# Running sums by way of device memory, and other orders for weights, fetches and norms in a two-layer kernel

## Chip, cores and metric

The kernel runs on one core of a Trainium2 chip. The metric is the device time of one execution in microseconds (us), taken as the median of the runs. The profile comes from one further execution of the same program.

## What is computed

Two layers work on x, 2 sequences of 512 tokens with 256 channels, all in float32. In each, x becomes x + s(norm(x)) * silu(f(norm(x))).

- Layer 0, s: a selective state-space scan. A root-mean-square norm and a projection give a gate (512 channels), the scan's input (512), a step width for each of 4 heads, and B and C (128 states). The input passes a causal convolution of width 4. Then, with running sums of the logarithmic decays, `L = exp(cum_i - cum_j)` for i >= j, `y = (L * (C B^T)) (dt x) + exp(cum) C state`, plus `D x`, times silu(gate), and an output projection.
- Layer 0, f: a mixture of 8 experts of which each token takes 2: `silu(x W1) * (x W2)`, then `W3`, weighted by the router's softmax.
- Layer 1, s: causal attention with 32 query heads, 8 key and value heads of 64 channels, and rotary positions.
- Layer 1, f: `sign(norm * gamma + beta)` times the signs of centred weights, plus a bias, times alpha.

## The kernel before

Tokens lie in 8 tiles of 128, 4 to a sequence (`b` is the sequence, `i0` the tile in it, `t` both). The program is one long order written out by hand (`manual_schedule`): each helper adds its instructions to the queues of the engines at the place where it is called, and each engine takes its own in that order. SyncE (SP) issues nearly all plain transfers and GpSimd (POOL) the indirect ones, each in order, so an issue that waits holds up those behind it.

*Layer 0.* After norms, routing and the first features (to about 40 us) the order mixes the experts with the scan. An expert ("unit") takes 256 token slots. Its rows are gathered from `rows` (`expert_slots`, L563), transposed (`expert_turned`, L594), multiplied by both up-projections in three calls of `expert_hidden` (L612) and projected by `expert_end` (L637), whose rows GpSimd scatters to the table `chosen` (L575). `weights_of(e)` asks for the up-projections `w` (two buffers, L358 and L359), `last_weights_of(e)` for `wp` (one buffer, L365). Before, `last_weights_of(e)` and `weights_of(e + 1)` are called behind `expert_end(e - 1)`. Tokens beyond the 256 of a unit go into an overflow block (`rests(0)`, the steps `next(few)`): its weights come as "pieces" by indirect gathers on GpSimd (L563), four to a piece, and are used in L707 and L739.

The scan goes by tile: `spread`, `decays`, `weighed`, `within`, `out_of`. `running_sums` makes the sums `cum` with one matmul of `la` (tokens by heads) by a triangle of ones (L444). `decays` needs the sums of a tile along the free axis, the same on all partitions. Before, `spread` multiplies the triangle by `la` on VectorE (L458, 128x512, two buffers `rl`), and a matmul by a matrix of ones adds the rows into PSUM:

```python
cps = bank_b()
cumb = heads(cps)
PE.matmul(cps, lhsT=ones, rhs=parts[t].rearrange("p h n -> p (h n)"), start=True, stop=True)
```

ScalarE (L471) and VectorE (L478, L481) read that. `spread` is called one to two tiles ahead of its `decays`.

*The turn* (about 224 to 254 us) leads from layer 0 to attention. `gates(1, ...)` (L258, L264) and a product (L1322) finish the scan's output of sequence 1 in `held`; `projected_out` multiplies it (L553), `scanned` adds it (L559). `fetched(b)` asks for the two expert rows of each token (`xn` L1090, `y1` L1091, four transfers of 256 KB on SyncE), `activated` adds them on GpSimd (L1098) and takes the silu on ScalarE (L1099). `residual` makes x and its moments on VectorE (L1104, L1105, L216), `begun1` takes square roots on ScalarE (L197, L198), `normed1_out` the norm on VectorE (L225), `features1` transposes it (L233) and copies it on ScalarE (L1124) to `x1T`. `weights_of_signs` transposes the signs (L1140) and copies them (L1141). `key` and `query` (L1169, rotation on VectorE) and `value` (L1186, copy L1188) follow. Attention's eight PSUM banks take the place of the ones used so far, and so its first scores (L1237) wait until those are free.

*Attention*, from about 254 us, goes head pair by head pair and is not edited.

Of the kernel before, what the change touches and what calls it, by code (L numbers as in the profile page):

```python
# [8 lines left out]
F32 = mybir.dt.float32  # L9
# [14 lines left out]

RESTS = 2 * (B * T - OWN) // REST
BLK = 2 * E + RESTS // RPB
MANY = 3
PIECE = 512
PIECES = 9
# [23 lines left out]
def fused_kernel(  # L53
# [35 lines left out]
    def bank_b():  # L89
        return psum.tile([P, 512], F32, tag="B", name="bank_b")  # L90
# [88 lines left out]
           allow_small_or_imprecise_dtypes=True)  # L179
    rows = dram.tile([B * T, C], F32, tag="rows", name="rows")  # L180
    chosen = dram.tile([2 * B * T, C], F32, tag="chosen", name="chosen")

    first = const.tile([P, NT, E], F32, tag="first", name="first")
    for e in range(E):
# [77 lines left out]
    def gates(b, which=range(NH)):  # L262
        for h in which:
            S.activation(gT[b][:, h, :], features(b, h * P, bank_a()), AF.Silu)  # L264
# [73 lines left out]
    def wide(name, t):  # L338
        return mw.tile([P, NH, P], F32, tag=name, name=f"{name}{t}")
# [16 lines left out]
    def weights_of(e):  # L356
        w = ep.tile([P, WID1], F32, tag="w", name=f"w{e}")
        nc.sync.dma_start(w[:, : 4 * PIECE].rearrange("p (n c) -> p n c", n=4), by_expert[e, :, :4])  # L358
        nc.sync.dma_start(w[:, 4 * PIECE :].rearrange("p (n c) -> p n c", n=2),  # L359
                          by_expert[e, :, 4:6, :384])  # L360
        weights[e] = [w]
# [79 lines left out]
    def running_sums():  # L441

        ps = bank_b()
        PE.matmul(ps[:, : NT * NH], lhsT=upper, rhs=la.rearrange("p t h -> p (t h)"),  # L444
                  start=True, stop=True)
        V.tensor_copy(cum.rearrange("p t h -> p (t h)"), ps[:, : NT * NH])

    def heads(ap):
        return ap.rearrange("p (h n) -> p h n", h=NH)
# [4 lines left out]
    def spread(b, i0):  # L454

        t = b * TPB + i0
        rl = wide("rl", t)
        V.tensor_tensor(rl, upper.unsqueeze(1).to_broadcast([P, NH, P]),  # L458
                        la[:, t, :].unsqueeze(2).to_broadcast([P, NH, P]), ALU.mult)
        parts[t] = rl  # L460

    def decays(b, i0):

        t = b * TPB + i0
        ti = slice(i0 * P, (i0 + 1) * P)

        cps = bank_b()
        cumb = heads(cps)
        PE.matmul(cps, lhsT=ones, rhs=parts[t].rearrange("p h n -> p (h n)"), start=True, stop=True)
        ec = wide("ec", t)  # L470
        S.activation(ec, cumb, AF.Exp)  # L471

        xps = bank_b()
        for h in range(NH):
            PE.transpose(xps[:, h * P : (h + 1) * P], ssmT[b][:, h, ti], ident)
        L = wide("L", t)
        for h in range(NH):
            V.scalar_tensor_tensor(L[:, h, :], cumb[:, h, :], cum[:, t, h : h + 1], negm,  # L478
                                   ALU.subtract, ALU.add)
        dte = mw.tile([P, NH], F32, tag="dte", name=f"dte{t}")  # L480
        V.tensor_tensor(dte, cumb[:, :, P - 1], cum[:, t, :], ALU.subtract)  # L481
        S.activation(L, L, AF.Exp)
        S.activation(dte, dte, AF.Exp)
        xdt = wide("xdt", t)
        V.tensor_tensor(xdt, heads(xps), dt3[:, t, :].unsqueeze(2).to_broadcast([P, NH, P]),
                        ALU.mult)
        parts[t] = ec, L, xdt, dte

    def weighed(b, i0):
        t = b * TPB + i0  # L490
        tk = slice(t * P, (t + 1) * P)
        ec, L, xdt, dte = parts[t]

        cb = bank_b()
        PE.matmul(cb[:, :P], lhsT=BT[:, tk], rhs=CT[:, tk], start=True, stop=True)
        V.tensor_tensor(L, cb[:, :P].unsqueeze(1).to_broadcast([P, NH, P]), L, ALU.mult)
        cs = xe = None
        if i0 < TPB - 1:
            xe = wide("xe", t)
            V.tensor_tensor(xe, xdt, dte.unsqueeze(2).to_broadcast([P, NH, P]), ALU.mult)  # L500
        if i0 > 0:
            cs = wide("cs", t)
            V.tensor_tensor(cs, CT[:, tk].unsqueeze(1).to_broadcast([P, NH, P]), ec, ALU.mult)
        parts[t] = (ec, L, xdt, cs, xe)
# [136 lines left out]
    def within(b, i0):  # L641
        outputs(b, i0)
        passed(b, i0)
        if b == 0:
            gated(b, i0)

    def out_of(b, i0):
        projected_out(b, i0)
        scanned(b, i0)
# [3 lines left out]
    def expert_slots(e):  # L653
        xgs[e] = gathered(e)

    def expert_turned(e):
        xgTs[e] = turned(e, xgs.pop(e))

    def expert_hidden(e, *groups):
        hidden(hids.setdefault(e, []), weights[e][0], xgTs[e], groups, e)  # L660

    def expert_end(e):
        project(e, weights[e], hids.pop(e))
# [95 lines left out]
    with tc.manual_schedule():  # L759
# [163 lines left out]
        convolved(0, 0)  # L923
        gates(0, (1,))
        running_sums()
        gates(0, (2,))
        expert_turned(0)
        expert_slots(1)
        spread(0, 0)
        gates(0, (3,))  # L930

        count = rt("count", [1], mybir.dt.int32)
# [21 lines left out]
        next(few)  # L954
        expert_hidden(1, 0)
        decays(0, 0)
        spread(0, 1)
        expert_end(0)
        last_weights_of(1)
        weights_of(2)  # L960
        weighed(0, 0)
        decays(0, 1)
        expert_hidden(1, 2)
        expert_turned(2)
        expert_slots(3)
        weighed(0, 1)
        within(0, 0)
        spread(0, 2)
        expert_hidden(1, 4)
        expert_hidden(2, 0)  # L970
        within(0, 1)
        decays(0, 2)
        expert_end(1)
        last_weights_of(2)
        weights_of(3)
        out_of(0, 0)
        weighed(0, 2)
        spread(0, 3)
        expert_hidden(2, 2)
        expert_turned(3)  # L980
        expert_slots(4)
        within(0, 2)
        expert_hidden(2, 4)
        decays(0, 3)
        out_of(0, 1)
        expert_hidden(3, 0)
        weighed(0, 3)
        expert_end(2)
        last_weights_of(3)
        weights_of(4)  # L990
        out_of(0, 2)
        conv_in(1, 0)
        within(0, 3)
# [12 lines left out]
        conv_in(1, 3)  # L1006
        convolved(1, 2)
        w_k, cs_t, w_f = early_weights()
        expert_end(3)
        last_weights_of(4)  # L1010
        weights_of(5)
        convolved(1, 3)
        spread(1, 0)
        expert_hidden(4, 2)
        decays(1, 0)
        expert_turned(5)
        expert_slots(6)
        expert_hidden(4, 4)
        next(few)
        weighed(1, 0)  # L1020
        spread(1, 1)
        expert_hidden(5, 0)
        within(1, 0)
        expert_end(4)
        last_weights_of(5)
        weights_of(6)
        next(few)
        decays(1, 1)
        expert_hidden(5, 2)
        weighed(1, 1)  # L1030
        expert_turned(6)
        expert_slots(7)
        expert_hidden(5, 4)
        within(1, 1)
        spread(1, 2)
        expert_hidden(6, 0)
        next(few)
        decays(1, 2)
        expert_end(5)
        last_weights_of(6)  # L1040
        weights_of(7)
        next(few)
        weighed(1, 2)
        expert_hidden(6, 2)
        next(few)
        expert_turned(7)
        spread(1, 3)
        expert_hidden(6, 4)
        next(few)
        within(1, 2)  # L1050
# [31 lines left out]
    w_q = aw.tile([P, KC, PAIRS * P], F32, tag="w_q", name="w_q", bufs=1)  # L1082
    x1 = x_sb

    def fetched(b):

        y1 = aw.tile([P, TPB, C], F32, tag=f"pr{b}", name=f"y1_{b}")
        by_tile = chosen.rearrange("(s p) c -> p s c", p=P)
        for t in range(b * TPB, (b + 1) * TPB, 2):
            nc.sync.dma_start(xn[:, t : t + 2, :], by_tile[:, t : t + 2, :])  # L1090
            nc.sync.dma_start(y1[:, t % TPB : t % TPB + 2, :], by_tile[:, NT + t : NT + t + 2, :])  # L1091
        return y1

    def activated(b, y1):
# [26 lines left out]
        normed(xn, x1, range(b * TPB, (b + 1) * TPB), mvs[b], made["roots", b][:, TPB:])  # L1121

    def features1(b):
        to_features(xn, b, lambda k, ps: S.copy(x1T[:, k, batch(b)], ps))  # L1124


    def signs_of_weights():
# [185 lines left out]

    tc.no_sync_barrier()
    with tc.manual_schedule():
        y1s = [fetched(0)]
        query_weights(0)
        signs_of_weights()
        within(1, 3)
        for h in range(NH):  # L1320
            gates(1, (h,))
            V.tensor_tensor(held[0][:, h, :], held[0][:, h, :], gT[1][:, h, :], ALU.mult)  # L1322
        w_v = mem.tile([P, KC, KV * HD], F32, tag="hT1", name="w_v")
        nc.sync.dma_start(w_v, wv.rearrange("(k p) n -> p k n", p=P))
        late_weights.append(w_v)
        query_weights(1)

        activated(0, y1s[0])
        for i0 in range(TPB):
            projected_out(1, i0)  # L1330
        made["wsT"] = weights_of_signs()
        mvs = [moments_of(0, "ln1")]
        for t in range(TPB):
            residual(t, mvs[0])
        begun1(0)
        normed1_out(0)
        for i0 in range(TPB):
            scanned(1, i0)
        y1s.append(fetched(1))
        features1(0)  # L1340
        activated(1, y1s[1])
        key(0, 0)
        nextq = query(0, 0)
        for i in range(2):
            value(0, i)
        mvs.append(moments_of(1, "ln1"))
# [220 lines left out]
```

## Time and profile before

| | |
|---|---|
| runs | 627.05, 627.86, 630.6 us; median 627.86 |
| profiled execution | 626.98 us, span 625.2 us |
| granted TensorE clock, mean | 0.997 |
| transfers | 45.74 MB; 73 GB/s over the span |
| ones-matmuls of the sums (L469) | 16 records (8 matmuls of two passes), 56.3 to 209.6 us |
| products for them on VectorE (L458) | 8, median 0.684 us |
| `w` transfers (1024 + 384 KB) | 8.9 to 11.8 us from issue to landing |
| `wp` transfers (768 KB) | 4.3 us from issue to landing |

The span runs from the first to the last instruction. PE is TensorE's matmuls and PEld its weight loads, DVE is VectorE, ACT ScalarE, POOL GpSimd; a float32 matmul appears as two records, one for each pass. "A <- B" behind an idle time names what ended it. "issue" is time in which the engine waited for nothing that the profile shows. The granted clock is TensorE's share of its full speed.

### The profile page before, as it was taken

The page shows a single profiled execution, that of the slowest core. Times are in us where ns is not written, and L with a number is a line of the kernel's source. Part 1 is how long each engine was busy: PE and PEld are TensorE (multiplying, and loading weights), DVE is VectorE, ACT ScalarE, POOL GpSimd, SP SyncE. Part 2 cuts the span into 40 slices and gives each one's busy share as a digit, 9 for nine tenths or more (in the row PEclk, how much of TensorE's full clock was granted, in tenths as well). Part 3 has the DMA queues.
Part 4 walks back from the last instruction along what each step waited for, and adds up shares of the span by engine and source line. Part 5 has one row for each costly group of instructions (what it writes and reads, how often), then busy time and mean ns, then how long its engine had stood idle before and what let it go on. Part 6 is the DMA issues. An engine that isn't in the chain of part 4 may idle for free.

```text
span 625.2 us, 11011 instructions
## 1 busy us (share of the span) xinstructions
PE 602.9 (96%) x3847; PEld 410.0 (66%) x3847; DVE 422.7 (68%) x1347; ACT 356.3 (57%) x921; POOL 278.7 (45%) x312
## 2 busy tenths in 40 slices
PE   7999999999998997999899999999999999999997
PEld 5568788777766864465455565666866656666676
DVE  6778654465435336899996889986159888888411
ACT  6443333243331434779888677886048999999610
POOL 3022411354663121575736537474025776666700
PEclk9999999999999998999999999999999999999999
DMA  7710641675856144000000000400000000000000
GB/s 240 266 35 24 230 150 38 221 228 196 282 165 227 72 159 160 2 1 2 1 2 2 0 2 1 135 2 1 18 17 2 2 2 1 3 2 1 2 11 23
DMA packets 24987, 45.74 MB, mean 73 GB/s; under 512 B 2621, under 2 KB 12607, under 8 KB 24928
## 3 DMA queue, kind: packets, MB, share of 16 engines
q1 hardware_dynamic: 19840, 30.71, 14.2%
q0 software_dynamic: 4512, 13.77, 7.2%
q8 instruction: 31, 0.51, 0.3%
q10 hardware_dynamic: 576, 0.52, 0.2%
q14 instruction: 28, 0.23, 0.1%
HBM read 40.80 MB, written 4.33 MB: 72 GB/s over the span
## 4 chain that ended last, share of the span: by engine, by line
PE 48%; DVE 13%; ACT 4%; issue 1%; POOL 1%; DVEq 0%; POOLq 0%; ACTq 0%
PE bank L1296 9%; PE bank L1288 8%; PE bank L1169 7%; PE bank L1276 7%; PE bank L1237 7%; DVE pr L1250 5%; PE bank_a L637 2%; ACT pr L1256 2%; PE bank L1186 1%; POOL pr L1264 1%; PE bank_a L258 1%; DVE sw_q L1159 1%; PE bank_a L612 1%; PE bank_b L553 1%; PE bank L1148 1%
## 5 line engine op out<-in xcount | busy, mean ns | idle before, releaser
L1264 POOL TENSOR_SCALAR pr<-pr,den 128x128 f32<-128x128 f32 (+2 forms) x192 | 193.7, 1024 | 145.1 <-DVE den L1432 145.1
L1256 ACT ACTIVATE pr<-pr,nmax 128x128 f32<-128x128 f32 (+3 forms) x256 | 142.3, 562 | 44.7 <-DVE nmax L1250 43.3
L1250 DVE CUSTOM_DVE_ANT_0 pr<-bank,cmask 128x128 f32<-128x128 f32 (+3 forms) x256 | 109.8, 484 | 11.0 <-PE bank L1237 7.3
L1277 ACT COPY pt<-bank 128x384 f32<-128x384 f32 (+1 forms) x192 | 82.3, 525 | 12.6 <-PE bank L1276 12.6
L1276 PEld LDWEIGHTS bank<-ident,pr 128*128 128x128 f32 x640 | 71.6, 141 | 20.4 <-issue 12.2
L612 PE MATMUL bank_a<-xgT,w 128*128 128x256 f32 x352 | 79.7, 379 | 0.9 <-DMA w<-in_moe 0.9
L1276 PE MATMUL bank<-ident,pr 128*128 128x128 f32 x640 | 75.6, 273 | 2.8 <-DVE oT L1416 2.3
L1288 PE MATMUL bank<-pt,v 128*64 128x384 f32 (+3 forms) x512 | 77.0, 439 | 1.4 <-ACT pt L1277 1.4
L612 PEld LDWEIGHTS bank_a<-xgT,w 128*128 128x128 f32 x352 | 65.5, 190 | 10.4 <-DVE yg L542 1.2
L1237 PE MATMUL bank<-kT,q 64*64 64x128 f32 (+7 forms) x1024 | 69.9, 410 | 0.7 <-ACT v L1188 0.7
L1288 PEld LDWEIGHTS bank<-pt,v 128*64 128x64 f32 x512 | 35.6, 136 | 46.1 <-issue 22.1
L1169 PE MATMUL bank<-x1T,w_q 128*128 128x512 f32 x124 | 61.5, 618 | 0.0
L1296 PE MATMUL bank<-w_o,oT 128*128 128x256 f32 x256 | 56.1, 380 | 0.6 <-DVE oT L1413 0.6
L1296 PEld LDWEIGHTS bank<-w_o,oT 128*128 128x128 f32 x256 | 48.3, 190 | 7.7 <-DVE oT L1413 0.8
L1256 ACT ACTIVATION_READ_ACCUMULATOR pr<-pr,nmax 128x1 f32 x256 | 50.3, 197 | 0.0
L1237 PEld LDWEIGHTS bank<-kT,q 64*64 64x64 f32 x1024 | 38.0, 133 | 14.3 <-issue 5.1
L563 POOL DMA_INDIRECT piece<-in_moe,wrow x36 | 37.4, 1040 | 22.2 <-issue 9.4
L1169 PEld LDWEIGHTS bank<-x1T,w_q 128*128 128x128 f32 x124 | 21.0, 189 | 37.0 <-issue 27.0
L575 POOL DMA_INDIRECT chosen<-o,dest x16 | 16.4, 1024 | 64.7 <-ACT o L574 34.8
L637 PE MATMUL bank_a<-wp,hid 128*128 128x256 f32 x192 | 43.1, 380 | 0.3 <-PEq L1065 0.3
L563 POOL DMA_INDIRECT xg<-rows,tok x16 | 16.7, 1046 | 54.0 <-DVE res L917 29.2
L637 PEld LDWEIGHTS bank_a<-wp,hid 128*128 128x128 f32 x192 | 35.9, 190 | 6.1 <-issue 1.6
(282 smaller groups left out, 794.6 us busy)
## 6 DMA issues: line engine op xcount, KB each, us to landing
w<-in_moe SPq DMA_DIRECT2D x8, 1024.0 KB, 11.8
wp<-in_moe SPq DMA_DIRECT2D x8, 768.0 KB, 4.3
w<-in_moe SPq DMA_DIRECT2D x8, 384.0 KB, 8.9
w_q<-in_wq SPq DMA_DIRECT2D x2, 1024.0 KB
w_o<-in_wo SPq DMA_DIRECT2D x2, 1024.0 KB
rows<-xn SPq DMA_DIRECT2D x4, 256.0 KB, 3.1
xn<-chosen SPq DMA_DIRECT2D x4, 256.0 KB, 2.8
y<-chosen SPq DMA_DIRECT2D x4, 256.0 KB, 3.0
```

The source lines that it names most:

```text
L563: G.indirect_dma_start(out=buf, out_offset=None, in_=src[:, :], in_offset=bass.IndirectOffsetOnAxis(ap=at, axis=0), bounds_check=src.shape ...
L612: PE.matmul(ps[:, i * OWN : (i + 1) * OWN], lhsT=w[:, a : a + P], rhs=xgT[:, k * OWN : (k + 1) * OWN], start=(k == 0), stop=(k == KC - 1))
L637: PE.matmul(ps[:, :C], lhsT=hid[j // 2][:, a : a + P], rhs=wp[:, j * C : (j + 1) * C], start=(j == 0), stop=(j == 5))
L1169: PE.matmul(ps, lhsT=w[:, k, n * P : (n + 1) * P], rhs=x1T[:, k, batch(b)], start=(k == 0), stop=(k == KC - 1))
L1237: PE.matmul(pss[hh][to, a : a + full], lhsT=q[half, n * HD : (n + 1) * HD], rhs=kT[b][half, m, :full], start=True, stop=True)
L1250: V.tensor_tensor_reduce(w["pr"][hh][:, span(i)], w["ps"][i][hh], cmask[:, i & 1, T - (i + 1) * P :], -1.0, 3.0e38, ALU.add, ALU.min, w["n ...
L1256: S.activation(x, x, AF.Exp, scale=-1.0, bias=w["nmax"][hh][:, i : i + 1], accum_out=sum_of(w, i, hh))
L1264: eng.tensor_scalar(x, x, sum_of(w, i, hh), None, ALU.mult)
L1276: PE.transpose(ps[:, col : col + P], pr[hh][:, at : at + P], ident)
L1277: S.copy(pts[hh][:, bank_at[n] : bank_at[n] + widths[n]], ps[:, : widths[n]])
L1288: PE.matmul(pv[hh * HD : (hh + 1) * HD, j * P :], lhsT=v_sb[b][:, j, g * HD : (g + 1) * HD], rhs=pts[hh][:, at : at + w], start=(j == 0), ...
L1296: PE.matmul(ps[:, :C], lhsT=oTs[b][:, c, i * P : (i + 1) * P], rhs=made["w_o"][c // 8][:, c % 8, :], start=(c == 0), stop=(c == PAIRS - 1))
```

## The change

1. The sums of a tile no longer come from VectorE and TensorE. `running_sums` makes them a second time with tile and head on the partitions (32x128) and writes them to a table `cum_rows` in device memory; `spread` reads one row of 512 numbers to all 128 partitions by a transfer on SyncE. `spread` is called two tiles ahead, right behind the `decays` that frees its buffer.
2. `weights_of(e)` is called ahead of `expert_end(e - 2)` instead of behind it and behind `last_weights_of(e - 1)`; `expert_hidden(1, 4)` moves ahead of `weighed(0, 1)` and `within(0, 0)`.
3. In the turn, `fetched(0)` is called behind the first gate, with `y1` on ScalarE's queue; `weights_of_signs` is called ahead of the silus and of `projected_out`; two matmuls of constants, whose result nobody reads, stand behind `projected_out`; `features1(0)` goes ahead of `scanned` and `fetched(1)`, and its second copy to VectorE.

```diff
+KEEP = 2
...
+    cum_rows = dram.tile([NT * NH, P], F32, tag="cum_rows", name="cum_rows")
...
+        PE.matmul(ps[: NT * NH, P : 2 * P], lhsT=la.rearrange("p t h -> p (t h)"), rhs=upper,
+                  start=True, stop=True)
+        by_row = lent("yg", "by_row", P)[: NT * NH]
+        V.tensor_copy(by_row, ps[: NT * NH, P : 2 * P])
+        nc.sync.dma_start(cum_rows[:, :], by_row)
         V.tensor_copy(cum.rearrange("p t h -> p (t h)"), ps[:, : NT * NH])
...
     def spread(b, i0):
         t = b * TPB + i0
-        rl = wide("rl", t)
-        V.tensor_tensor(rl, upper.unsqueeze(1).to_broadcast([P, NH, P]),
-                        la[:, t, :].unsqueeze(2).to_broadcast([P, NH, P]), ALU.mult)
-        parts[t] = rl
+        cumb = wide("rl", t)
+        nc.sync.dma_start(cumb.rearrange("p h n -> p (h n)"),
+                          cum_rows[t * NH : (t + 1) * NH, :].rearrange("a n -> (a n)")
+                          .partition_broadcast(P))
+        parts[t] = cumb
...
     def decays(b, i0):
-        cps = bank_b()
-        cumb = heads(cps)
-        PE.matmul(cps, lhsT=ones, rhs=parts[t].rearrange("p h n -> p (h n)"), start=True, stop=True)
+        cumb = parts[t]
...
         running_sums()
+        spread(0, 0)
+        spread(0, 1)
         gates(0, (2,))
         expert_turned(0)
         expert_slots(1)
-        spread(0, 0)
...
         decays(0, 0)
-        spread(0, 1)
+        spread(0, 2)
+        weights_of(2)
         expert_end(0)
         last_weights_of(1)
-        weights_of(2)
         weighed(0, 0)
         decays(0, 1)
+        spread(0, 3)
         expert_hidden(1, 2)
         expert_turned(2)
         expert_slots(3)
+        expert_hidden(1, 4)
         weighed(0, 1)
         within(0, 0)
-        spread(0, 2)
-        expert_hidden(1, 4)
         expert_hidden(2, 0)
         within(0, 1)
         decays(0, 2)
+        spread(1, 0)
+        weights_of(3)
         expert_end(1)
         last_weights_of(2)
-        weights_of(3)
...
         w_k, cs_t, w_f = early_weights()
+        weights_of(5)
         expert_end(3)
         last_weights_of(4)
-        weights_of(5)
         convolved(1, 3)
-        spread(1, 0)
         expert_hidden(4, 2)
         decays(1, 0)
+        spread(1, 2)
...
-    def fetched(b):
+    def fetched(b, second=nc.sync):
...
             nc.sync.dma_start(xn[:, t : t + 2, :], by_tile[:, t : t + 2, :])
-            nc.sync.dma_start(y1[:, t % TPB : t % TPB + 2, :], by_tile[:, NT + t : NT + t + 2, :])
+            second.dma_start(y1[:, t % TPB : t % TPB + 2, :], by_tile[:, NT + t : NT + t + 2, :])
...
     def features1(b):
-        to_features(xn, b, lambda k, ps: S.copy(x1T[:, k, batch(b)], ps))
+        to_features(xn, b, lambda k, ps: (S.copy, V.tensor_copy)[k if b == 0 else 0](
+            x1T[:, k, batch(b)], ps))
...
     with tc.manual_schedule():
-        y1s = [fetched(0)]
-        query_weights(0)
         signs_of_weights()
         within(1, 3)
         for h in range(NH):
             gates(1, (h,))
+            if h == 0:
+                y1s = [fetched(0, nc.scalar)]
+                query_weights(0)
             V.tensor_tensor(held[0][:, h, :], held[0][:, h, :], gT[1][:, h, :], ALU.mult)
...
         query_weights(1)
+        made["wsT"] = weights_of_signs()
         activated(0, y1s[0])
         for i0 in range(TPB):
             projected_out(1, i0)
-        made["wsT"] = weights_of_signs()
+        ps = bank_a()
+        for _ in range(KEEP):
+            PE.matmul(ps, lhsT=ident, rhs=cmask[:, 0, :], start=True, stop=True)
         mvs = [moments_of(0, "ln1")]
         for t in range(TPB):
             residual(t, mvs[0])
         begun1(0)
         normed1_out(0)
+        features1(0)
         for i0 in range(TPB):
             scanned(1, i0)
         y1s.append(fetched(1))
-        features1(0)
         activated(1, y1s[1])
         key(0, 0)
```

The calls of `spread`, `weights_of`, `expert_end` and `last_weights_of` for the other tiles and units move in the same way.

## The prediction

> **What bounds the kernel.** I read the page's busy table, then TensorE's waits up to the start of attention, then the chain of work that ended last, then the timeline of the turn between the layers.
>
> ```profile
> PE 602.9 (96%) x3847; PEld 410.0 (66%) x3847; DVE 422.7 (68%) x1347; ACT 356.3 (57%) x921; POOL 278.7 (45%) x312
> ```
>
> TensorE is the bound, but an average hides where. Its waits between 20 and 254 us (total, times, longest):
>
> ```profile
> PE bank_a L233 <- issue: 4.1, 1, 4.1
> PE bank_b L739 <- DMA piece<-in_moe,wrow: 1.3, 2, 0.7
> PE bank_a L612 <- DMA w<-in_moe: 0.9, 1, 0.9
> PE bank L1237 <- ACT v L1188: 0.7, 1, 0.7
> ...
> PE bank_b L469 <- DVE rl L458: 0.4, 1, 0.4
> ```
>
> Before the turn (to 238 us) the listed idle time is about 4 us in 218: there, a matmul removed is time saved. In the turn TensorE stands for 4.1 us and waits on chains of other engines. The end of the turn in the chain (start, length, what):
>
> ```profile
> 238.79 0.58 ACT rw L1141
> 239.38 0.01 issue
> 239.38 1.28 ACT L197
> ...
> 242.75 1.98 PE bank_a L233 x8
> 244.73 5.00 PE bank_b L1169 x8
> 249.73 3.45 PE bank_b L1186 x8
> 253.18 0.02 issue
> 253.20 0.59 ACT v L1188
> ```
>
> Four passes should take 1.73 us (a later row of the same line has 1.91), yet the eight at 244.73 took 5.00: the windows (PE, PEld, DVE, ACT, POOL, granted clock, DMA share, GB/s) show why.
>
> ```profile
> 238.00:243.00 5.00, 0.94 (x7) 0.52 (x5) 3.51 (x16) 2.35 (x4) 0.00 (x0) 1.00 0.03 10
> 244.00:247.25 3.25, 3.25 (x8) 1.50 (x6) 0.94 (x3) 1.34 (x3) 0.00 (x0) 0.50 0.50 162
> ```
>
> After the idle stretch the clock is 0.50 from 244.0 to about 247.4.
>
> **Part 1: the sums.** Eight ones-matmuls (L469) go; the chain prices one:
>
> ```profile
> 209.35 0.86 PE bank_b L469 x2
> ```
>
> 8 x 0.86 = **-6.88 us**, all before the turn. The wait in front of one of them (0.42) goes too: **-0.42**. Eight VectorE products (L458, 0.684 us each) go from an engine that is off the path there: nothing. Added in `running_sums`: one matmul of two 128-column passes, 0.22 us by the spacing of the like pairs of L495: **+0.22**. Its 32x128 copy (the 128x32 copy beside it took 0.183) and the 16 KB write are hidden: the write can go at about 40 us, the first broadcast is wanted by `decays(0,0)` at 58, and SyncE issues nothing else between 19 and 62.
>
> The eight broadcasts of 256 KB are in no row of before. Nearest rows: `rows<-xn`, 256 KB, 3.1 us to landing; at the far end the 128 KB scatter at 186.15 that held its successor 7.6 us. I take 3, since shape and size are those of the first. Each is asked for two tiles ahead (`spread(0,2)` after `decays(0,0)`, 61.2, used near 80), so its latency is covered. Each waits on SyncE's queue for the decays that frees its buffer, with the next unit's weights queued behind: that is its real price, counted next. Reading the sums from SBUF instead of PSUM I price at nothing (ScalarE 0.597 from PSUM in L471, 0.630 from SBUF in L482: 8 x 0.03 on an engine with slack).
>
> **Part 2: unit weights sooner.** Before, `w` of unit e went behind `wp` of e-1, which waits for `expert_end`:
>
> ```profile
> 62.94 0.37 SPq L365 DMA_DIRECT2D wp<-in_moe  x1
> 63.42 0.42 SPq L358 DMA_DIRECT2D w<-in_moe  x1
> ```
>
> It was needed at 72.89 and came 0.86 late, 10.3 us after issue. Now it goes behind `spread(0,2)`, at about 61.7; TensorE needs it at 72.89 - 2 x 0.86 = 71.2. 61.7 + 10.3 = 72.0, less what `wp` no longer takes ahead of it. I take **-0.6** (bounds 0 and -0.86). Units 3, 4, 6 and 7 are asked 2.5 to 17 us sooner by the same reading, so they have cover; unit 5 (1.4 MB) stands behind the 0.75 MB that `early_weights` asks for at 132, and is needed at 146.9: 14 us for what the windows there move in 9.
>
> The last pieces of the overflow block waited 0.60 and 0.74 us. GpSimd shows why:
>
> ```profile
> 186.15 1.02 POOL L575 DMA_INDIRECT chosen<-o,dest  x1 [0.30 <-issue]
> 193.76 1.00 POOL L575 DMA_INDIRECT chosen<-o,dest  x1 [6.59 <-issue]
> 195.07 1.04 POOL L563 DMA_INDIRECT piece<-in_moe,wrow  x1 [0.30 <-issue]
> ```
>
> The second scatter waits while the DMA engines are full (share 1.02 from 188 to 192, the weights of unit 7, asked at 184.8), and the last gathers stand behind it. Those weights now move about 17 us earlier: **-1.0** (bounds 0 and -1.34). Against it: gathers of pieces 4 and 5 are eight issues 1.3 us apart from 160.2, and end just in time at 174.7; TensorE now comes 0.86 sooner: **+0.5** (bounds 0 and 0.9). `expert_hidden(1,4)` ahead of `weighed(0,1)` costs nothing: what slides back 2.8 us is first used at 86.4 (L553).
>
> Sum before the turn: -6.88 - 0.42 + 0.22 - 0.6 - 1.0 + 0.5 = **-8.2**.
>
> **Part 3: the turn**, on before's clock.
> - `y` on ScalarE's queue, behind the first gate (ends 226.46). Before, SyncE issued `xn` at 226.17 and `y` only at 227.20; now about 226.95. The two issues (0.4 each) delay the second gate by under 0.3, which the third absorbs. GpSimd's first add (231.82) comes up to 0.5 sooner.
> - The sign transposes (0.43) go between the gates and `projected_out`, into a 0.52 hole (waiting for `held`): nothing. Their copy (L1141, 0.58) now stands ahead of the first silu, until 232.2; so the residuals start at about 232.9 instead of 233.39, and end near 239.2 instead of 239.77.
> - The square root's table load (L197, 1.28) no longer waits for that copy: the root follows the moments by 0.1 instead of 0.9. Norms end at about 242.2 instead of 243.62: 1.4 sooner.
> - Two constant matmuls (128x512, 0.86 each) run from 238.1 to 239.9: no cost, since TensorE waits until 241.3 anyway. They shorten its idle time from 4.05 to 1.4, so I expect a clock of 1.0 for keys and queries.
> - The second feature copy goes to VectorE (0.68 beside ScalarE's 0.57). Keys then end near 245.0, and the values' passes at 250.2 instead of 253.17: 3.0 sooner.
>
> But **what is late next**: `fetched(1)` now follows `features1` and `scanned`. VectorE first waits for the transposes and copies (1.5 us), then makes the first two sums (0.72): 242.2 + 2.2 = 244.4, against 244.31 before. From there nothing is shortened:
>
> ```profile
> 250.13 1.84 POOL L1098 TENSOR_TENSOR xn<-xn,y 128x256 f32<-128x256 f32 x2 [0.82 <-DVE sw_k L1163]
> ```
> ```profile
> 252.00 0.42 ACT L1099 ACTIVATE xn<-xn 128x256 f32<-128x256 f32 x1 [0.27 <-POOL xn L1098]
> 252.32 0.57 ACT L1188 COPY v<-bank_b 128x512 f32<-128x512 f32 x1
> 253.20 0.58 ACT L1188 COPY v<-bank_b 128x512 f32<-128x512 f32 x1 [0.31 <-PE bank_b L1186]
> ```
>
> Both copies of `v` stand behind the four silus on ScalarE, and the first scores (L1237) waited for the second copy, since attention's banks reuse these. With values early, the copies can follow each other: 252.4 + 1.1 = 253.5 against 253.84. So the turn gives **-0.3**, of 3.0 that TensorE and VectorE could use. Bounds: -3.0 (the fetch lands as early as the values) and +1.4 (clock, below).
>
> The Trainium skill, "DMA: Bandwidth & Descriptors", "Issuing engines are not separate DMA queues", says that copies from several issuers share the same DMA engines and only issue time is saved. By that the first add gains at most the issue gap in the rows; with no gain at all the turn would be about +0.2 instead of -0.3.
>
> Attention itself is not edited; all shifts.
>
> **Sum.** -8.2 - 0.3 = -8.5. The profiled execution took 626.98 (span 625.2, 1.8 around it): 618.5. The median of the runs, 627.86, is 0.9 above it; I add half: **618.9**.
>
> **Rivals.**
> 1. *The clock falls before attention.* TensorE ends the values at 250.2 and would stand until 253.5: 3.3 us, against the 4.05 that ended in half clock here. For it: that length; against: idle 1.3 us at 6.7 left the clock at 1.00, and 3.3 is the shorter. Half clock for the observed 3.4 us costs 1.7, and the early heads are on TensorE in the chain: **620.6**. The Trainium skill, "TensorE: Matmul & The Clock Gate", "Part 1: The HAM clock gate", has a free-running window of about 3.4 us; the trace agrees in length (0.50 from 244.0 to 247.4), and by it this falls to the phase.
> 2. *The turn pays in full*, if the second fetch lands sooner than I read: -3.0, **616.2**. Against: its four transfers took from 244.31 to about 250.
> 3. *The gathers become the bound* from 145 to 203: the stall of 1.34 stays, and the two sums removed there (1.72) are largely given back: -8.5 + 1.0 + 1.6 = -5.9, **621.5**. For it: GpSimd issues back to back from 160 to 173 and 176 to 187; against: the DMA engines have less to do in the second.
> 4. *Slower: the broadcasts are dear*, 128 reads of one 2 KB row. A broadcast of p us holds unit 2's weights back by p - 1 and unit 3's by p - 4 (cover of 4); no gain is left from p = 6.8, over 0.5% is lost from p = 8.3; at 9, 13 us: **632**. For it, only that no row has one; against, 2.8 to 3.1 us for the nearest shapes.
>
> That the change does not do what it says has a part in the first two: constants may hold the clock where it no longer counts.
>
> **Chances.** Forecast 0.45, rivals 0.20, 0.12, 0.15, 0.08. The range takes in the first three rivals, 615.3 to 622.4. About 0.5% (3 us) is what a measurement of this kernel tells from no change: faster by more 0.87 (forecast and rivals 1 to 3, less 0.05 for several together), within 0.06, slower 0.07.
>
> **What would show it.** No ones-matmul; TensorE's first scores near 245.3 of the span; no wait of L612 on `w`; pieces' waits under 0.5; clock 1.0 between norms and scores, with scores released by ScalarE's copy of `v`. Wrong if a `w` lands late behind a broadcast, if the last gathers still stand behind a scatter, or if the scores start when the values end.

## The result and the profile after

The changed kernel takes 620.72 us (median of 6 runs, 619.05 to 623.05), the kernel before beside it 627.45 (626.69 to 630.6): a ratio of 0.990 with a 95% interval of 0.9876 to 0.9924, so about 1% faster. The profiled execution took 620.49, with a span of 618.5.

Page of the changed kernel, busy times:

```profile
PE 598.7 (97%) x3837; PEld 407.9 (66%) x3837; DVE 420.1 (68%) x1341; ACT 355.8 (58%) x920; POOL 278.5 (45%) x312
```

TensorE is 4.2 us less busy, not the 6.9 of the matmuls that went: the two constant matmuls (1.9) and the added one (about 0.4) make up most of the difference. Its waits from 20 to 250 us (total, times, longest):

```profile
PE bank_a L235 <- issue: 1.8, 1, 1.8
PE bank_b L714 <- DMA piece<-in_moe,wrow: 1.2, 2, 0.9
PE bank_b L1177 <- DVE s L566: 1.2, 1, 1.2
PE bank L1245 <- ACT v L1196: 0.7, 1, 0.7
PE bank_b L746 <- DMA piece<-in_moe,wrow: 0.6, 1, 0.6
```

The waits for `w` and for `rl` are gone. The last pieces (L746) wait once, not twice, but the gathers ahead of them (L714) wait 1.2, and there is a wait that was not forecast: the keys (L1177) wait for `scanned` (L566).

Two marks, the first gate of the turn and the first scores of attention, cut the span into three parts (us). Attention, which was not edited, has the same length:

| | before | after | difference | forecast |
|---|---|---|---|---|
| first gate of the turn | 223.94 | 216.49 | -7.45 | -8.2 |
| from there to the first scores | 29.90 | 30.48 | +0.58 | -0.3 |
| from there to the end | 371.4 | 371.5 | +0.1 | 0 |

The end of the turn in the changed kernel's chain (start, length, what):

```profile
234.59 1.71 PE bank_a L235 x8
...
236.93 0.42 DVE s L566
237.35 0.14 issue
237.49 5.37 PE bank_b L1177 x8
242.86 3.45 PE bank_b L1194 x8
246.31 0.02 issue
246.33 0.59 ACT v L1196
246.92 0.04 issue
246.97 1.18 PE bank L1245 x17
```

The keys' and queries' passes take 5.37 us, as in before (5.00), though constants had kept TensorE busy ahead of the norms. The windows show the cause (the third number from the end is the granted clock):

```profile
236.00:238.00 2.00, 0.80 (x4) 0.34 (x3) 1.68 (x5) 0.47 (x1) 0.00 (x0) 0.97 0.00 0
238.00:240.00 2.00, 2.00 (x4) 0.88 (x3) 0.34 (x2) 0.00 (x0) 0.00 (x0) 0.50 0.49 141
240.00:242.00 2.00, 2.00 (x5) 0.82 (x4) 1.10 (x3) 1.28 (x1) 0.54 (x1) 0.67 0.96 276
```

Half clock from 237.9 to about 241.3 is 3.4 us long, as before; two shorter idle stretches (1.76 and 1.20) stand ahead of it instead of one of 4.05. So the chain to the first scores runs through the values at half clock: they end at 246.31, and the last silu only 0.55 sooner, at 245.76.

### The profile page after: what moved, and what is told of

It reads as the page before. It is cut to its first block, busy times and chain, and to the rows that moved or that the text cites. A ratio compares the mean times of both kernels' runs of the same rounds, so it can differ in the third digit from the quotient of the medians.

```text
span 618.5 us, 11000 instructions
## 1 busy us (share of the span) xinstructions
PE 598.7 (97%) x3837; PEld 407.9 (66%) x3837; DVE 420.1 (68%) x1341; ACT 355.8 (58%) x920; POOL 278.5 (45%) x312
## 4 chain that ended last, share of the span: by engine, by line
PE 51%; DVE 11%; ACT 2%; issue 1%; POOL 1%; DMA 1%; ACTq 0%; DVEq 0%; POOLq 0%
PE bank L1296 10%; PE bank L1304 9%; PE bank L1177 8%; PE bank L1245 8%; PE bank L1284 8%; DVE pr L1258 4%; PE bank_a L644 2%; PE bank L1194 1%; POOL pr L1272 1%; PE bank L1156 1%; PE bank_a L619 1%; DVE sw_q L1167 1%; PE bank_b L1177 1%; DVE q L1168 1%; ACT pr L1264 1%
## 5 line engine op out<-in xcount | busy, mean ns | idle before, releaser
L1177 PE MATMUL bank<-x1T,w_q 128*128 128x512 f32 x124 | 61.5, 618 | 0.0
L1177 PEld LDWEIGHTS bank<-x1T,w_q 128*128 128x128 f32 x124 | 21.0, 189 | 37.0 <-issue 27.0
L644 PE MATMUL bank_a<-wp,hid 128*128 128x256 f32 x192 | 42.9, 380 | 0.6 <-PEq L1072 0.3
L644 PEld LDWEIGHTS bank_a<-wp,hid 128*128 128x128 f32 x192 | 36.0, 190 | 6.3 <-issue 1.2
```

The source lines that it names most:

```text
L644: PE.matmul(ps[:, :C], lhsT=hid[j // 2][:, a : a + P], rhs=wp[:, j * C : (j + 1) * C], start=(j == 0), stop=(j == 5))
L1177: PE.matmul(ps, lhsT=w[:, k, n * P : (n + 1) * P], rhs=x1T[:, k, batch(b)], start=(k == 0), stop=(k == KC - 1))
```

## The experiments

Theory A: the gain is made ahead of the turn; the turn's edits bring nothing, because the second fetch still sets the first scores and the keys' bank and the clock take what the norms gained. Rival B: the turn pays. Rival C: the order of calls does not matter and the half clock does. In the table, "turn" is the time from the first gate to the first scores (us), and every run has a kernel of before beside it (medians 626.47 to 627.76).

| kernel | median | ratio, 95% interval | first gate | turn | clock in the turn |
|---|---|---|---|---|---|
| e1_head | 619.23 | 0.9875 [0.9844, 0.9907] | 215.73 | 30.46 | half from norms |
| e2_turn | 628.96 | 1.0027 [1.0003, 1.0052] | 223.14 | 30.02 | half at keys |
| e5_scan_first | 617.3 | 0.9844 [0.9806, 0.9882] | 216.01 | 28.13 | full |
| e6_early_rows | 618.42 | 0.9859 [0.9824, 0.9893] | 216.62 | 29.58 | half from norms |
| e7_no_constants | 617.67 | 0.9831 [0.9802, 0.9861] | 215.59 | 29.02 | half at keys |
| e8_rows_behind_weights | 617.65 | 0.9839 [0.9795, 0.9884] | 214.26 | 29.55 | half at keys |
| e9_one_queue | 619.46 | 0.9857 [0.9826, 0.9887] | 215.47 | 31.09 | half at scores |
| e10_sums_alone | 624.74 | 0.9949 [0.9926, 0.9972] | 221.04 | 30.68 | half from norms |
| e11_weights_alone | 625.7 | 0.9966 [0.995, 0.9983] | 221.27 | 30.20 | half from norms |
| e12_vector_adds | 617.62 | 0.9821 [0.9794, 0.9849] | 215.26 | 29.59 | half at keys |
| e13_three_constants | 615.53 | 0.9822 [0.9797, 0.9848] | 214.43 | 27.35 | full |
| e14_after_three | 619.9 | 0.9885 [0.9858, 0.9912] | 214.48 | 29.78 | half at keys |

First gate, turn and clock come from one profiled execution each. Nine of these profiles and the one of the changed kernel share the same head, and their first gate lies anywhere from 214.26 to 216.62: it goes with what TensorE waited for gathered pieces (L714 and L746 together): 0.2 to 0.4 us in the three earliest, 1.8 and 2.1 in the two latest. So a turn is read from its own length, and medians under half a per cent apart are not ranked.

### Head or turn

**e1_head**: the changed kernel with the turn of before.

```diff
-        signs_of_weights()
+        y1s = [fetched(0)]
+        query_weights(0)
+        signs_of_weights()
...
-            if h == 0:
-                y1s = [fetched(0, nc.scalar)]
-                query_weights(0)
...
-        ps = bank_a()
-        for _ in range(KEEP):
-            PE.matmul(ps, lhsT=ident, rhs=cmask[:, 0, :], start=True, stop=True)
```

> Sums through device memory and weights sooner alone; the turn as it was before. Theory A (all of the gain lies ahead of the turn, and the turn's edits as a whole cost some 0.6 us): the first gate of the turn starts at 216.5 us of the span as in the changed kernel, gate to first scores takes 29.9 us as before, span 617.9, about 0.6 below the changed kernel. Rival B (the turn's edits pay, and the time was lost elsewhere): the turn is longer than the 30.5 us of the changed kernel, span 619 or more.

**e2_turn**: the kernel before with the hunks of the turn alone (the same lines the other way).

> The turn's edits alone; sums and weights as before. Theory A: first gate at 223.9 us of the span, gate to first scores 30.5 us (0.6 more than before), span 625.8, so no gain. Rival B: under 29.9 us in the turn and a span under 625.

The head alone has the whole gain, and 619.23 is no slower than both together. The turn's edits alone are 0.27% slower (interval 0.03% to 0.52%). In e2 the wait of the keys appears at once:

```profile
243.71 3.57 PE L1171 MATMUL bank_b<-x1T,w_k 128*128 128x512 f32 x4 [1.20 <-DVE s L560]
```

That falls to theory A. Its sum of the turn's cost (0.6) is not measured closely: e1 and e2 have turns of 30.46 and 30.02, in the wrong order for it.

### What holds the turn

**e5_scan_first**: scan and second fetch ahead of the features, both feature copies on ScalarE.

```diff
-        features1(0)
         for i0 in range(TPB):
             scanned(1, i0)
         y1s.append(fetched(1))
+        features1(0)
```

> The changed kernel with one part of the turn undone: the four sums of scanned and the second fetch ahead of the feature transposes again, both feature copies on ScalarE. Theory A (what is late next is the second fetch, and the keys wait for PSUM banks that scanned frees): the second fetch is asked for about 1.5 us sooner, the keys' wait of 1.20 us goes, the scores start 1.2 us sooner, gate to scores 29.3 us, span 617.3. Rival C (the order does not matter, the clock at half speed does): gate to scores stays at 30.3 to 30.7 us.

The keys' wait is 0.24 instead of 1.20, the second fetch is asked 2.2 us sooner (19.05 after the first gate, not 21.21), the clock stays full, and the turn is 28.13: better than either expectation. The order matters, against rival C. Scores still wait, and ScalarE's rows say for what:

```profile
242.03 0.42 ACT L1106 ACTIVATE xn<-xn 128x256 f32<-128x256 f32 x1 [1.15 <-POOL xn L1105]
242.72 0.42 ACT L1106 ACTIVATE xn<-xn 128x256 f32<-128x256 f32 x1 [0.27 <-POOL xn L1105]
243.04 1.05 ACT L1195 COPY v<-bank_b 128x512 f32<-128x512 f32 x2
```

The values are through at 242.6; both copies of `v` stand behind the last silus, which wait for GpSimd, which waits for the second fetch. That is the chain that the prediction named.

**e6_early_rows**: e5, and the second fetch into buffers of its own, asked behind the second gate.

```diff
+            if h == 1:
+                y1s.append(fetched1())
```

> As the run before, and the second fetch goes to buffers of its own, asked for right behind the second gate, so that it waits for nothing. Theory A: no fetch on the path any more, the scores start when the values are copied: 27.8 us from gate to scores with a full clock at the keys, 29.5 us with 3.4 us at half clock; span 615.8 to 617.5. Rival C: the same 30.3 to 30.7 us, if the fetch was never what the scores waited for.

The silus are done before the values, but the transfers stand in the way of the first fetch. Adds 3 and 4 on GpSimd:

```profile
228.73 1.41 POOL L1105 TENSOR_TENSOR xn<-xn,y 128x256 f32<-128x256 f32 x2 [3.13 <-DMA y<-chosen]
```

The norms come late, the idle stretch is 3.00, and the clock falls: 29.58, the upper expectation.

**e8_rows_behind_weights**: the same fetch, asked behind `query_weights(1)`.

> e5_scan_first, with the second fetch into buffers of its own as in e6_early_rows, but asked on SyncE behind the weights of queries and values instead of behind the second gate. Theory A (the second fetch's chain holds the first scores, and e6 lost that only because its transfers stood in the way of the first fetch): adds 3 and 4 start as in e5, clock 1.00, the silus are done ahead of the values, the copies of v follow the values at once; the wait of 1.59 us ahead of the scores shrinks to about 0.65, turn 27.2, median 616.3. Rival B (the transfers are in the way wherever they are asked): norms late as in e6, turn 29.5, median 618.5. Rival C (the values, not the silus, set the scores): turn 28.1, median 617.3.

Rival B has the length of the turn (29.5 against 29.55), but not the reason; A and C miss. The first fetch is no more disturbed than in e5, but GpSimd's sums of the second one run while VectorE makes the norms (first row GpSimd, second VectorE; in e5 the second took 1.38):

```profile
231.49 2.97 POOL L1120 TENSOR_TENSOR x<-x,y 128x256 f32<-128x256 f32 x4 [4.86 <-DMA y<-chosen]
```
```profile
231.22 2.65 DVE L227 TENSOR_SCALAR xn<-x_sb,ln_mv,ln_r 128x256 f32<-128x256 f32 x4
```

**e12_vector_adds**: those sums on VectorE, behind the scan.

```diff
-            G.tensor_tensor(x2[:, i, :], x2[:, i, :], y2[:, i, :], ALU.add)
+            V.tensor_tensor(x2[:, i, :], x2[:, i, :], y2[:, i, :], ALU.add)
```

> e8_rows_behind_weights with the four sums of the second fetch on VectorE behind the scan instead of GpSimd, nothing else. In e8 the GpSimd sums ran from 231.5 beside VectorE's norms, which took 2.65 us for four instead of 1.38, and TensorE waited 1.2 for them. Theory A (that neighbour is what spoilt e8): norms' transposes without those waits, keys start 19.5 after the first gate, clock 1.00, silus done by 22.5, copies of v follow the values, turn 27.2, span 614.5, median 616.3. Rival B (the clock falls in any case after the idle stretch): turn 29, median 618. Rival C (the extra 1.7 us on VectorE delay the rotation of keys and queries): turn 28, median 617.1.

```profile
233.03 1.39 DVE L227 TENSOR_SCALAR xn<-x_sb,ln_mv,ln_r 128x256 f32<-128x256 f32 x4
```

The norms take 1.39 again and the sums 1.42, so the neighbour is confirmed. But the clock fell after 1.66 us of idle time, so the turn is 29.59 (rival B). Its executions lie in two groups, and the mean granted clock of each execution goes with them: 615.0 and 615.07 us at 0.999 and 1.000, 617.62 to 618.24 us at 0.996 to 0.997.

### The clock and the constants

**e7_no_constants**: e5 with `KEEP = 0`.

> e5_scan_first without its two constant matmuls (KEEP = 0), nothing else. Theory A (the constants hold the clock there: with them TensorE's idle stretch ahead of the keys is 1.4 us and the clock stays 1.00): without them TensorE stands some 3.2 us between projected_out and the norms' transposes, the clock falls to 0.50 for 3.4 us and the turn takes 28.1 + 1.7 = 29.8 us; median 619.0. Rival B (the constants do nothing, the order of the scan alone kept the clock): clock 1.00, turn 28.1, median 617.3.

The clock falls in the profile, as theory A has it, but costs 0.9 (29.02 against 28.13), not 1.7: the rest hides in the wait for the second fetch. The medians do not tell the two apart (617.67 and 617.3), but the mean granted clocks do: 0.993 to 0.997 in all four executions without the constants, 0.999 or 1.000 in three of the four with them (e5). So the constants hold the clock in most executions, and the time that this saves is too small to see here.

**e13_three_constants**: e12 with `KEEP = 3`.

> e12_vector_adds with a third constant matmul (KEEP = 3), nothing else. In e12 the clock still fell, to 0.50 for some 3.4 us, after an idle stretch of 1.66 us and a wait of 0.24, and the copies of v followed the values 1.4 us later than at full clock; in e5 it held after 1.40. Theory A (the length of the idle stretch decides, and one more pair of passes of 0.86 closes it to 0.8): clock 1.00 through the turn, turn 27.6 to 27.9, span 614.4, and the executions gather near 615.2 instead of lying between 615.0 and 618.2. Rival B (the constants do not count for the clock, its phase decides): clock 0.50 in the profile or not by chance, median 617.6. Rival C (the third constant delays the norms' transposes): turn longer by up to 0.9.

The idle stretch is 0.66, the clock full, and the chain has nothing left in it but TensorE and two copies:

```profile
221.90 6.91 PE bank_b L560 x32
228.81 2.58 PE bank_a L1359 x6
231.38 0.66 issue
232.04 1.27 PE bank_a L235 x4
233.31 0.02 issue
233.33 0.59 ACT x1T L1146
233.93 0.04 issue
233.97 3.70 PE bank_b L1191 x8
237.67 3.45 PE bank_b L1208 x8
241.12 0.02 issue
241.14 0.59 ACT v L1210
```

The turn is 27.35, a little shorter than theory A had it. Five of the six executions have a mean granted clock of 1.000 (615.0 to 616.08 us); one has 0.996 and takes 616.85. This kernel has the shortest turn and the lowest median of the study.

**e14_after_three**: the changed kernel with `KEEP = 3`.

> The changed kernel with a third constant matmul (KEEP = 3), nothing else. Theory A (the first scores wait for the second fetch, whatever the clock does at the keys): clock 1.00 at the keys, values ready 1.7 us sooner, and the wait ahead of the scores grows from 0.68 to over 2 us; turn 30.4, median 620.5 within 0.7, or 1.7 more where the longer wait lets the clock fall in attention. Rival B (the half clock at the keys is what the turn lost): turn 28.8, median 618.9.

The expectation of a full clock was wrong: the idle stretch was only 0.46, but the keys still waited 1.21 for the scan, and the clock fell behind that. 619.9 is within what theory A gave, but as the condition did not come about, this run does not decide between the two. With the keys' wait left in, a third constant does not buy the clock: the mean granted clock is 0.994 to 0.997 in five of the six executions.

### One queue or two

**e9_one_queue**: the changed kernel with `y` back on SyncE.

```diff
-                y1s = [fetched(0, nc.scalar)]
+                y1s = [fetched(0)]
```

> The changed kernel with the rows y of the first sequence back on SyncE's queue, all else as changed. Theory A (the second queue brings the first add 0.5 us sooner, and loses it again in adds 3 and 4, where y's second half shares the DMA engines with the query weights): first add 0.4 later relative to the first gate, adds 3 and 4 without their wait of 1.25, second gate 0.3 sooner; norms within 0.3, median 620.7 within 0.5. Rival B (the second queue pays): norms 0.5 later, median 621.2 or more. Rival C (the second queue harms): norms 0.7 sooner and, with a shorter idle stretch, a full clock: median 618.6.

The norms' transposes start 18.02 after the first gate, against 18.10: the second queue brings nothing. Theory A has the result, not its parts: the first add is 0.14 later, not 0.4, and adds 3 and 4 still wait 1.04 for `y`, though `y` now stands ahead of the query weights on the same queue. Here the clock was full at the keys, and the scores came no sooner; they waited longer for the copies behind the silus, and then the clock fell in attention:

```profile
246.56 3.65 PE L1245 MATMUL bank<-kT,q 64*64 64x128 f32 x32 [3.06 <-ACT v L1196]
```

In the profile of the changed kernel that wait is 0.68, and the same 32 passes take 2.38 at full clock. So in the changed kernel a full clock at the keys is worth nothing: with it, the second fetch decides.

### Sums or weights

**e10_sums_alone**: e1 with the weights asked for where they were before the change. The cut shows unit 2; units 3 to 7 move in the same way.

```diff
-        weights_of(2)
         expert_end(0)
         last_weights_of(1)
+        weights_of(2)
```

> Only the sums through device memory: e1_head with the unit weights asked for where they were before the change, and the turn as before. Theory A (by the positions of the changed kernel: w of unit 2 late by 0.86, pieces late by 1.34 instead of 0.60, but the gathers of pieces 4 and 5 have the 0.86 more): first gate 215.7 + 0.9 + 0.7 = 217.3 at the latest, turn 30.5, span 619.1, median 620.8. Rival B (the weights sooner bring nothing that the gathers do not take back): median 619.3. Rival C (the removed matmuls only deepen the waits for weights): gate 218.5, median 622.

**e11_weights_alone**: the kernel before with `weights_of` moved forward for units 2 to 7, and nothing else (the same lines the other way).

> Only the unit weights sooner: the kernel before, with weights_of(k) ahead of expert_end(k-2) for units 2 to 7, sums and turn as before. It completes a table of four: neither 223.9 (first gate of the turn), sums alone 221.0, both 215.7. Theory A (removing a matmul uncovers a transfer: the sums alone lost to waits for weights what these edits give back, so the two are not additive): here the weights can take away only the waits that before shows, 0.86 for w and up to 1.34 for the last pieces: gate 221.7 to 223.1, turn 29.9, median 625.8 (625.2 to 627). Rival B (the weights sooner are worth 5.3 us by themselves, as between sums alone and both): gate 218.6, median 622.3.

e10 is slower than all three expectations; e11 has the median of theory A, with the first gate 0.4 sooner than its range. The first gate stands at 223.94 with neither edit, 221.04 with the sums alone (-2.90), 221.27 with the weights alone (-2.67) and 215.73 with both, in e1 (-8.21): 2.6 more than the two alone add up to. Each is one profile, and the first gate varies by up to 2.4 in the ten of one head; but the medians, each against the kernel of before beside it, agree: -3.02, -1.83 and -8.17. One thing is not the same in the two cases: in e11 `w` of unit 2 is asked for at 53.06, in e1 at 62.03, behind a broadcast on SyncE that waits until its buffer is free. Waits of TensorE with the sums alone:

```profile
PE bank_a L619 <- DMA w<-in_moe: 2.6, 1, 2.6
PE bank_b L746 <- DMA piece<-in_moe,wrow: 2.5, 4, 0.8
```

Before, these were 0.9 and 1.3. The first cost more than its length, since the clock fell behind it (before, then the sums alone):

```profile
73.75 3.69 PE L612 MATMUL bank_a<-xgT,w 128*128 128x256 f32 x16 [0.86 <-DMA w<-in_moe]
```
```profile
74.64 5.38 PE L619 MATMUL bank_a<-xgT,w 128*128 128x256 f32 x16 [2.60 <-DMA w<-in_moe]
```

The same 16 passes take 1.7 more. The account: -6.88 for the matmuls, +0.4 for the added one, (2.6 + 2.5) - (0.9 + 1.3) = +2.9 of waits for transfers, +1.7 of half clock, -0.4 for `rl`, -0.3 each for a wait on `hrT` and one of L707, +0.3 for one on `hid` is -2.6; -2.90 was measured. In e11 the waits that go sum to 1.9 of the 2.67; the rest stays open.

## Why the prediction was right, and where it was not

The direction and the range held; the forecast of 618.9 was 1.8 low. By the profiled executions 618.5 was forecast and 620.49 measured: +0.75 ahead of the turn, +0.88 in it, +0.1 in attention, +0.3 outside the span.

Of its own signs, the missing wait of L612 came true. The first scores at 246.97 (not 245.3), the pieces' waits (0.60 and 1.21, not under 0.5) and the clock between norms and scores did not. One sign of being wrong, scores that start when the values end, did show: the half clock made the values late (246.31), and the scores followed.

**Part 1, the sums.** -6.88 stands as work removed, but "all before the turn" holds only together with part 2: alone, the sums gave 2.90. The added matmul was priced at 0.22 and took 0.33 to 0.43. The first ones-matmul had covered a silu; without it L644 waits 0.26 for `hid`, which no step priced. The wait for `rl` went as forecast. The broadcasts are not dear: SyncE issues one in 0.32 to 0.38, the median from issue to landing is 3.9 us in e1 and 4.0 in e10 where 3 was taken, and TensorE waits for none. In e10 `w` of unit 2, asked at the same time as before, came 0.9 later (74.64 against 73.75), with two broadcasts among its transfers; that these are the cause was not tested by itself.

**Part 2, the weights.** Here the attribution failed. "I take -0.6 (bounds 0 and -0.86)" and "-1.0 (bounds 0 and -1.34)" price the weights by the waits that the trace of before shows. Each was about right as a difference between the two kernels: TensorE no longer waits for `w` (-0.86), and the pieces gave -0.74. But the sums' removal makes the deadlines earlier, and once the sums are removed the weights are worth 5.3 us, the step from e10 to e1 (221.04 to 215.73). The sum used the new deadline for `w` of unit 2 (71.2), and so came out near the right total; it did not say that without this edit more than half of the other one would be lost (2.90 left of 7.08).

**Gathers** of pieces 4 and 5 were to cost 0.5 (bounds 0 and 0.9): 1.21 of waits, where before had 0.34, make 0.87, near the bound. This is rival 3 in part, and it varies: over the ten profiles of this head the first gate is at 215.4 on average, 8.1 ahead of the mean of before and e2 (223.94 and 223.14). So the forecast of -8.2 was better than the one profile of the changed kernel makes it look.

**Part 3, the turn.** "What is late next" was right as the limit: with a full clock at the keys (e9) the scores wait for the second fetch and do not come sooner. In the profile of the changed kernel the values at half clock come 0.55 behind the last silu and hide that. Three steps inside it were wrong.
- *"Keys then end near 245.0"*: the keys' bank was overlooked. `projected_out` leaves its sums in PSUM until `scanned` has read them, and with the features called ahead of it VectorE reads them last, behind its own feature copy. The new wait is 1.20, in after, e2, e9 and e14; in e5, with the scan first, 0.24 for another engine is all.
- *"I expect a clock of 1.0 for keys and queries"*: it was 0.50 for 3.4 us. The keys' wait made a second idle stretch. Rival 1 has the length and the price of half clock right (1.7), not the place; that its 620.6 lies next to the measured 620.72 is luck, since by e9 a full clock at the keys would have gained nothing.
- *First add up to 0.5 sooner, residuals from 232.9*: the first add did come 0.46 sooner (7.42 after the first gate, not 7.88). But adds 3 and 4 then waited 1.25 for the second half of `y`, which moved beside the query weights. That the second queue let these in is not the whole cause, as 1.04 of the wait is left in e9; the cause stays open. VectorE also ran beside GpSimd's sums. In the chain of the changed kernel three of its rows are about twice as long as their like:

```profile
225.12 0.94 DVE xn L1111
...
227.19 0.85 DVE xn L1111
...
228.06 0.85 DVE x_sb L1112
...
229.49 0.42 DVE xn L1111
...
229.94 0.43 DVE x_sb L1112
```

The moments end 15.99 after the first gate, before the change 15.83. Only the earlier table load was kept: the norms end 18.98 after the gate, not 19.68. The Trainium skill, "DMA: Bandwidth & Descriptors", "Issuing engines are not separate DMA queues", was cited against this gain, and e9 agrees with it: 0.08 us between one queue and two.

**Rivals.** 2 (the turn pays) is refuted by e1 and e2; what it promised is there, but needs scan, fetch and sums in another order and a third constant: e13 has 27.35. 4 (dear broadcasts) is refuted by the landing times above and by TensorE's list of waits, which has none for them.

## What to carry to other kernels

Where transfers are only just on time, an edit that takes work from the bounding engine and one that asks for data sooner are worth their price only together; price the second against the deadlines that the first leaves. When calls change places, ask which PSUM bank each one frees and who takes it next, and which engine now runs beside another and slows it. Of an expected clock, count every idle stretch up to the work that needs it, not the longest alone, and expect executions to differ.

## What was not expected of the hardware

- The granted clock does not follow from the length of one idle stretch. Ahead of the keys, 1.40 and 0.24 us left it at 1.00 (e5), and so did 1.54 and 1.21 (e9, full through keys and queries); 0.46 and 1.21 did not (e14). A drop lasted 3.41 us each time, or twice that ahead of the keys in e10 and e11 (6.83). The Trainium skill, "TensorE: Matmul & The Clock Gate", "Part 1: The HAM clock gate", has a free-running window of about 3.4 us and names one idle window as what lowers the clock. The length of a drop agrees; the condition, read as a window without any work, does not: in e14 no stretch of idle time in the turn is longer than 1.21 us.
- The phase of such a window can be read from the traces. Within a profile the clock falls at times that lie whole multiples of 3.413 us apart (e10: 74.66 and 238.50, 48 of them). Counted back from the drops, both idle stretches of e14 lie in the one window ahead of its drop; in e9 they lie in two, and the clock held behind both (e14, then e9):

```profile
231.42:234.83 3.41, 1.74 (x10) 1.02 (x9) 2.55 (x7) 0.58 (x1) 0.00 (x0) 1.00 0.00 0
234.83:238.24 3.41, 3.41 (x4) 1.40 (x5) 0.80 (x3) 0.35 (x1) 0.00 (x0) 0.50 0.58 171
```
```profile
230.46:233.88 3.42, 1.88 (x6) 0.63 (x4) 2.87 (x13) 0.49 (x2) 0.00 (x0) 1.00 0.02 10
233.88:237.29 3.41, 2.20 (x9) 1.18 (x10) 2.50 (x7) 0.58 (x1) 0.00 (x0) 1.00 0.00 0
237.29:240.70 3.41, 3.41 (x9) 1.52 (x8) 2.27 (x5) 1.28 (x1) 0.42 (x1) 1.00 0.69 222
```

- So where the idle time falls against the window separates e9 from e14. TensorE's busy time in a window is still not the whole condition: the changed kernel's clock fell behind a window with 2.09 us of it (234.47 to 237.89), and e9's held behind 1.88. What counts as busy stays open, and no run sets the phase by itself.
- Some VectorE operations on 128x256 float32 take about twice as long beside GpSimd sums: four norms 2.65 us instead of 1.38, single sums 0.85 instead of 0.42. The statistics of the moments do not: 0.43 beside them too (before, at 234.78). The Trainium skill, "SBUF — State Buffer", section "SBUF: two separate sides", has the two engines lock a shared pair of ports for a whole instruction, VectorE for some kinds of operation only; these rows agree.
- Eight reads of one 2 KB row by 128 partitions each, 256 KB, took 3.9 us to landing in e1 (median; 3.1 to 10.8), and TensorE waits for none of them.
